# A gated layer's inverse deviation by Newton steps on VectorE, and two attentions whose ends are interleaved

## The chip, the cores and the metric

The kernel runs on one core of a Trainium2 chip. The metric is the device time in microseconds, median of the runs. PE is the matrix engine, DVE the vector engine, ACT the scalar engine, POOL the GpSimd engine; SP issues nearly all DMAs.

## What is computed

The input x has 4 batches of 512 rows of 256 numbers (f32). Four residual layers follow one another, each on the layer norm of x:

```
x = x + attn_a(ln(x))      # 16 heads of 128, causal softmax, biases
x = x + gated(ln(x))       # per head: o normalised by its own mean and variance, times silu(g)
x = x + attn_b(ln(x))      # 16 heads, low-rank queries, keys and values, rotary part, causal softmax
x = x + gated(ln(x))       # the same weights again
```

What matters of the gated layer (it mixes the four batches per position) is its end:

```
mu = mean(o, axis=-1); var = var(o, axis=-1)        # 16 heads of 16 numbers
o = (o - mu) / sqrt(var + EPS)
out = (silu(g) * o.reshape(b, l, d)) @ Wout
```

## The kernel before

The order of all work is written out by hand: every engine and every DMA queue runs its instructions in the order in which the program emits them, and the program waits only where data or a buffer demands it.

The main line is `attention_full`: 64 units (4 batches of 16 heads) in a loop of steps i = 0 to 66, a software pipeline. Step i scores unit i (four matmuls `score`, L282; mask and row maximum on DVE, L290; exponential on ACT, L293), transposes the probabilities of unit i-1 (32x32 blocks on DVE, L317, `turn`; then `carry`, L328 and L331: one DMA to DRAM, `way`, and four back), projects queries and keys of unit i+1 (L256), divides by the row sum on POOL (L308), multiplies by the values for unit i-2 (`mix`, L344) and adds a quarter of an older group of four heads to x (`output`, L366, L373). `load(i)` issues the weights of coming heads on SP, behind `carry`. So steps 64, 65 and 66 have no scores: they finish what is in the pipeline.

`attention_lowrank` is the second attention: 64 units of its own (`loop`, u = 0 to 66), each with four scores of growing width (L984), mask (L992), exponential (L995), division on POOL (L1011), transposes on PE (L1019) with copies to `probsT`, values (L1043), output (L1063). Its rotary parts are made by `rotated`: two products on DVE (L899, L900), two copies on ACT (L901, L902), then a shuffle on DVE (L905) and two sums on POOL (L906, L907). `compress_queries` (L915), `compress_keys` (L928), `compress_values` (L943) and `project` (L961) make its operands; `prologue(stage)` makes the first ones within steps 48 and 63 to 66 of the first attention, reading tables that `lowrank_weights` left in DRAM. PSUM has two buffers for such results (`ps_mm`).

Beside the main line run two lanes of generators, `norms` and `work`. Each call of `beside()` advances the first job of `norms`, or, when that is empty, of `work`, up to its next `yield`. A step of the first attention calls it four times (six for batches 2 and 3); a unit of the second four times (eight in the last batch). In `work` are the weights' preparation (`gated_weights`, `lowrank_weights`) and the gated layers, each as two halves of two row tiles that alternate yield by yield. A `norm` takes statistics on DVE (L132), makes `rstd` by a power and `shift` on POOL (L136 to L140), writes normalised rows `xn` on POOL (L146), turns them on PE (L154) and copies them to `xT` (L156). The last norm and last gated layer have nothing beside them.

The end of a half of a gated layer: squares on ACT (L675), their sum and the variance on DVE (L678, L679), then the power -1/2 in place, on POOL, in four pieces of 8 columns (L685), each with its own `yield`; the product with the gate on POOL (L690); the product with the inverse deviation on DVE (L692); transposes (L698) and the output product (L706). For the last gated layer alone, `by_power=False` takes a square root on ACT (L688) and a reciprocal on DVE (L689).

Of the kernel before, what the change touches and what calls it, by code (L numbers as in the profile page):

```python
# [10 lines left out]

F32 = mybir.dt.float32
AF = mybir.ActivationFunctionType
ALU = mybir.AluOpType
# [4 lines left out]
P = 128  # L19
# [16 lines left out]
def network(ctx: ExitStack, tc: tile.TileContext, ins: dict, out: bass.AP):  # L36
# [35 lines left out]

    slots = dict(bo=D, mask=S, probs_0=S, probs_2=3 * S, val0=D, val1=D, turns=2 * S)
    for i in range(2):
# [52 lines left out]
    def norm(b, take, extra=None):  # L127

        stats = lnpool.tile([P, NT, 6], F32, name="stats")
        mv = lnpool.tile([P, NT, 2], F32, name="mv")  # L130
        for t in range(NT):
            nc.vector.bn_stats(stats[:, t, :], x[b][t])  # L132
            nc.vector.bn_aggr(mv[:, t, :], stats[:, t, :])
            yield
        rstd = lnpool.tile([P, NT], F32, name="rstd")
        nc.gpsimd.tensor_scalar(rstd, mv[:, :, 1], EPS, None, ALU.add)  # L136
        nc.gpsimd.tensor_tensor(rstd, rstd, minus_half[:, :NT], ALU.pow)
        shift = lnpool.tile([P, NT], F32, name="shift")
        nc.gpsimd.tensor_tensor(shift, mv[:, :, 0], rstd, ALU.mult)
        nc.gpsimd.tensor_scalar(shift, shift, -1.0, 1.0, ALU.mult, ALU.mult)  # L140
        yield
        xT = new_xT()

        def normalise(t):
            xn = lnpool.tile([P, D], F32, name="xn")
            nc.gpsimd.tensor_scalar(  # L146
                xn, x[b][t], rstd[:, t : t + 1], shift[:, t : t + 1], ALU.mult, ALU.add
            )
            return xn

        def transpose(t, xn):
            pt = ps_tp()
            for c in range(DC):
                nc.tensor.transpose(pt[:, c * P : (c + 1) * P], xn[:, c * P : (c + 1) * P], ident)  # L154
# [19 lines left out]
    def attention_full(events, prologue):  # L174
# [218 lines left out]
        take_bias(0)()  # L393
        for i in range(n + 3):
            b, h = divmod(i, H)
# [19 lines left out]
            load(i)  # L415
            if i >= n - 1:
                prologue(i - n)
            beside(2 if b > 1 else 1)
# [14 lines left out]
            if 0 <= g < groups:  # L433
                for tt in range(t, NT if i == n + 2 else t + 1):
                    output(g, tt)


# [76 lines left out]

    def gated(layer, l, xT, xT_before, half, after, by_power=True):

# [163 lines left out]
        yield  # L680
        if by_power:
            step = 8
            for n in range(0, HT * H, step):
                part_ = var[:, n : n + step]
                nc.gpsimd.tensor_tensor(part_, part_, minus_half[:, :step], ALU.pow)  # L685
                yield
        else:
            nc.scalar.activation(var, var, AF.Sqrt)  # L688
            nc.vector.reciprocal(var, var)  # L689
        nc.gpsimd.tensor_tensor(o, o, gate, ALU.mult)  # L690
        yield
        nc.vector.tensor_tensor(og, og, var.unsqueeze(2).to_broadcast([P, HT * H, HDV]), ALU.mult)  # L692
        yield
# [51 lines left out]
    def lowrank_weights():  # L745
# [5 lines left out]
        for o in range(OCT):  # L751
            heads = slice(8 * o, 8 * o + 8)
            for to, tag, name in ((wqT, "w0", "b_wqT"), (wkT, "w1", "b_wkT"), (wvT, "gd", "b_wvT")):
                to.append(wide(tag, o, name[2:], S).rearrange("p (h r) -> p h r", r=RANK))
                nc.sync.dma_start(to[o], ins[name][:, heads, :])
            yield
            queries.append(wide("cx", o, "wqb"))
            wq.append(queries[o].rearrange("r (p s k) -> r p s k", p=4, s=2))
        wout = []
        places = [("kv1", 1), ("kv2", 0), ("kv2", 1), ("kv3", 0), ("kv3", 1), ("q", 0)]  # L760
        for i, place in enumerate(places):
            h0, h1 = 3 * i, min(H, 3 * i + 3)
            part = wide(*place, "wout", (h1 - h0) * D).rearrange("p (h d) -> p h d", d=D)
            nc.sync.dma_start(part, ins["b_wout"][:, h0:h1, :])
            wout += [part[:, h - h0, :] for h in range(h0, h1)]
            if i % 2:
                yield


        for i in range(2):  # L770
            nc.sync.dma_start(wkv[:, :, 0, i, :], ins["b_wkva"][:, :, :RANK])
            for block in range(2):
                for odd in range(2):
# [4 lines left out]
                    other = (1 - odd) * 32 + block * 16  # L778
                    nc.sync.dma_start(sin[rows], ins["c_sin"][RANK + other : RANK + other + 16])
                    nc.sync.dma_start(  # L780
                        wkv[:, :, 1, i, to : to + 16], ins["b_wkva"][:, :, RANK + at : RANK + at + 16]
                    )
                yield
        for o in range(OCT):
            for i in range(2):
                for block in range(2):
                    for odd in range(2):
# [4 lines left out]
                        )  # L792
                yield
            ps = ps_mm()
# [37 lines left out]
    def attention_lowrank(xTs, events):  # L832
# [14 lines left out]
        def load_tables():  # L847
            cos, sin, wkv = slot("wq0", "cos"), slot("wq1", "sin"), slot("wk0", "wkv")
            nc.sync.dma_start(wkv, tables[:, 2 * S :])
            nc.sync.dma_start(cos, tables[:, :S])  # L850
            nc.sync.dma_start(sin, tables[:, S : 2 * S])
            wq = slot("wv0", "wqb")
            nc.sync.dma_start(wq, to_queries)
            lw["cos"], lw["sin"] = (a.rearrange("p (i q) -> p i q", q=32) for a in (cos, sin))
            lw["wkv"] = wkv.rearrange("p (c a i r) -> p c a i r", c=DC, a=2, i=2)
# [9 lines left out]
        def buffers():  # L865
# [7 lines left out]
            lw["probs"] = {}  # L873
            for t in (0, 2, 3):
                probs_of(t)

        def probs_of(t):
            tag = ("probs_0", "zT0", "probs_2", "probs1")[t]
            lw["probs"][t] = slot(tag, f"probs{t}", (t + 1) * S).rearrange("p (i k) -> p i k", i=4)
# [3 lines left out]
        def more_buffers():  # L883
            probs_of(1)

# [5 lines left out]
        def rotated(first, second, ps):  # L891
# [3 lines left out]
            rank, straight = (p.rearrange("p (i q) -> p i q", q=32) for p in ps)  # L895
            both = slot(("wv1", "turns")[turns[0] % 2], "turns")
            turns[0] += 1
            t1, t2 = (both[:, i * S : (i + 1) * S].rearrange("p (i q) -> p i q", q=32) for i in range(2))
            nc.vector.tensor_tensor(t1, straight, lw["cos"], ALU.mult)  # L899
# [11 lines left out]
        def compress_queries(b):  # L911
            qas[b] = slot("wk1", "qa")
            ps = ps_mm()
# [157 lines left out]

        def prologue(stage):
            if stage == -2:
                load_first()
            elif stage == -1:
                load_tables()
            elif stage == 0:
                compress_queries(0)
                compress_keys(0)
                buffers()  # L1080
            elif stage == 1:
                compress_values(0)
                for p in range(2):
                    project(0, 0, p)()
            elif stage == 2:
                for p in range(2, 4):
                    project(0, 0, p)()

        pair_at = {(4, 1): 0, (5, 0): 1, (5, 2): 2, (6, 1): 3}
        output_at = {(1, 1): 0, (1, 3): 1, (3, 0): 2, (3, 2): 3}  # L1090
        compress_at = {(9, 2): compress_queries, (10, 3): compress_keys, (11, 3): compress_values}

        def loop():
            load_last()
            more_buffers()
            later = []
            for u in range(n + 3):
                octet, j = divmod(u, 8)
                b, jb = divmod(u, per_batch)
                events(u, b, jb)  # L1100
                for i in range(4):
# [43 lines left out]

    def then_gated(layer, l, after=None, by_power=True):
        def take(xT):
            gated_in[layer][l] = xT
            halves = [
                gated(layer, l, xT, gated_in[layer].get(l - 1), half, after, by_power)  # L1150
                for half in range(2)
# [5 lines left out]
    def during_full(i, b, h):  # L1157
# [4 lines left out]
        if (b, h) == (B - 1, 0):  # L1162
            assert (0, 0) in complete
            norms.add(norm(0, keep_lowrank(0)))
            prologue(-2)
# [17 lines left out]
    run(norm(B - 1, then_gated(1, B - 1, store, by_power=False)))  # L1183
    while work.jobs:
# [82 lines left out]
```

## Time and profile before

| | us |
|---|---|
| three runs | 1517.03, 1517.52, 1520.23 |
| median | 1517.52 |
| the profiled execution | 1520.02 |
| its span, first to last instruction | 1518.3 |
| PE busy | 1343.7 (89%) |
| DVE busy | 831.7 (55%) |
| POOL busy | 643.6 (42%) |
| ACT busy | 573.6 (38%) |

The mean granted clock of PE is 0.944 of full speed. Busy shares are means over stages: the first attention fills the first 850 us or so, the second the next 600, and the last gated layer the rest. A line of the profile names engine, source line, operation, what is written and what is read; a bracket gives the idle time before it and what ended it. SPq is SP's DMA queue. A wait is put down to the producer that came last.

### The profile page before, as it was taken

To read this page: it belongs to the slowest core of one execution; us is meant where nothing else is said; L and a number is where in the kernel's file an instruction comes from. 1 tells how busy PE (TensorE), PEld (TensorE's weight loads), DVE (VectorE), ACT (ScalarE), POOL (GpSimd) and SP (SyncE) were. 2 spreads that over 40 slices of the span, in tenths; PEclk is the share of its full clock that TensorE was granted. 3 is DMA by queue.
4 is the path that set the end of the run, shared out by engine and by line. 5 is a ranking of instruction groups with operands and counts; after the bars stand their busy time and mean duration, and the time that the engine had idled before them with its cause. 6 is when DMAs were issued, how large, how long until landed. Compare 5 with 4: busy or idle time off the path is not lost.

```text
span 1518.3 us, 16974 instructions
## 1 busy us (share of the span) xinstructions
PE 1343.7 (89%) x4984; PEld 778.2 (51%) x4984; DVE 831.7 (55%) x2460; ACT 573.6 (38%) x1593; POOL 643.6 (42%) x1027
## 2 busy tenths in 40 slices
PE   7969999999999999999995879996999799778771
PEld 3535556556556555655553535453645455435441
DVE  3533555554655566556483464974456556647327
ACT  3422333333333333333331245554355546434321
POOL 3311123221163235313346362867353666756624
PEclk9989999999999999999997899998899999989785
DMA  2776656554554535545353000000000000000000
GB/s 95 205 240 165 200 157 172 171 150 130 161 167 139 162 119 171 165 139 152 113 155 101 28 1 0 1 2 0 1 1 1 1 15 1 1 14 1 14 1 14
DMA packets 88284, 133.80 MB, mean 88 GB/s; under 512 B 16128, under 2 KB 69888, under 8 KB 88192
## 3 DMA queue, kind: packets, MB, share of 16 engines
q1 hardware_dynamic: 88192, 132.72, 29.6%
q8 instruction: 40, 0.66, 0.2%
q14 instruction: 52, 0.43, 0.1%
HBM read 86.29 MB, written 46.40 MB: 87 GB/s over the span
## 4 chain that ended last, share of the span: by engine, by line
PE 74%; DVE 9%; POOL 8%; DMA 3%; issue 3%; ACT 1%; SPq 1%; POOLq 0%; ACTq 0%; DVEq 0%
PE ps_mm L256 14%; PE ps_pz L344 9%; PE ps_sc L282 8%; PE ps_mm L243 7%; PE ps_mm L366 7%; PE ps_sc L984 6%; PE ps_mm L549 6%; PE ps_pz L1043 4%; PE ps_mm L1063 3%; PE ps_tp L1019 3%; PE ps_mm L706 2%; PE ps_mm L961 2%; POOL var L685 2%; POOL probs L1011 2%; PE ps_tp L154 1%
## 5 line engine op out<-in xcount | busy, mean ns | idle before, releaser
L308 POOL TENSOR_SCALAR probs<-probs,inv 128x128 f32<-128x128 f32 (+3 forms) x256 | 132.8, 537 | 492.4 <-DVE inv L305 444.5
L293 ACT ACTIVATE probs<-ps_sc,nmax 128x128 f32<-128x128 f32 (+3 forms) x256 | 134.8, 527 | 284.2 <-DVE nmax L290 260.8
L995 ACT ACTIVATE probs<-ps_sc,nmax 128x32 f32<-128x32 f32 (+15 forms) x256 | 124.6, 488 | 257.8 <-DVE nmax L992 185.8
L1011 POOL TENSOR_SCALAR probs<-probs,inv 128x32 f32<-128x32 f32 (+15 forms) x256 | 128.9, 521 | 146.0 <-DVE inv L1008 100.6
L984 PE MATMUL ps_sc<-kTb,qTb 128*128 128x160 f32 (+15 forms) x512 | 179.9, 443 | 9.5 <-ACT probs L995 8.2
L992 DVE CUSTOM_DVE_ANT_0 ps_sc<-ps_sc,mask_b 128x32 f32<-128x32 f32 (+15 forms) x256 | 112.9, 444 | 102.5 <-PE ps_sc L984 76.5
L282 PE MATMUL ps_sc<-kT,qT 128*128 128x128 f32 (+3 forms) x512 | 159.9, 435 | 1.9 <-DVE inv L305 0.9
L290 DVE CUSTOM_DVE_ANT_0 ps_sc<-ps_sc,mask_a 128x128 f32<-128x128 f32 (+3 forms) x256 | 126.4, 500 | 53.2 <-PE ps_sc L282 52.3
L344 PE MATMUL ps_pz<-probsT,v 128*128 128x512 f32 (+3 forms) x512 | 150.8, 438 | 3.1 <-DVE var L679 1.8
L984 PEld LDWEIGHTS ps_sc<-kTb,qTb 128*128 128x128 f32 x512 | 86.3, 201 | 105.4 <-issue 58.3
L344 PEld LDWEIGHTS ps_pz<-probsT,v 128*128 128x128 f32 x512 | 97.8, 192 | 82.4 <-issue 58.9
L256 PE MATMUL ps_mm<-xT,wk 128*128 128x512 f32 x256 | 122.8, 603 | 13.4 <-DMA wk<-in_a_wk_dram 13.4
L357 DVE TENSOR_SCALAR zT<-ps_pz,bias 128x512 f32<-128x512 f32 x64 | 48.0, 751 | 153.2 <-PE ps_pz L344 153.1
L243 PE MATMUL ps_mm<-wv,xT 128*128 128x512 f32 x256 | 122.4, 603 | 0.0
L256 PE MATMUL ps_mm<-xT,wq 128*128 128x512 f32 x256 | 121.7, 598 | 0.0
L366 PE MATMUL ps_mm<-wo,zT 128*128 128x256 f32 x512 | 120.8, 380 | 0.0
L317 DVE STREAM_TRANSPOSE squares<-probs 128x512 f32<-128x512 f32 (+3 forms) x256 | 115.0, 487 | 0.0
L1019 PE MATMUL ps_tp<-ident,probs 128*128 128x128 f32 x640 | 104.9, 289 | 11.1 <-ACT probsT L1028 7.2
L282 PEld LDWEIGHTS ps_sc<-kT,qT 128*128 128x128 f32 x512 | 86.2, 191 | 36.1 <-issue 26.9
L366 PEld LDWEIGHTS ps_mm<-wo,zT 128*128 128x128 f32 x512 | 94.0, 190 | 17.2 <-issue 6.7
L549 PE MATMUL ps_mm<-w_in,cx 128*128 128x512 f32 (+1 forms) x256 | 96.2, 509 | 6.0 <-DVE cx L540 4.7
L1019 PEld LDWEIGHTS ps_tp<-ident,probs 128*128 128x128 f32 x640 | 82.3, 152 | 37.3 <-issue 12.7
(141 smaller groups left out, 2020.2 us busy)
## 6 DMA issues: line engine op xcount, KB each, us to landing
way<-squares SPq DMA_DIRECT2D x64, 640.0 KB, 2.9
probsT<-way SPq DMA_DIRECT2D x256, 160.0 KB, 3.3
wv<-in_a_wv_dram SPq DMA_DIRECT2D x16, 512.0 KB, 5.1
wq<-in_a_wq_dram SPq DMA_DIRECT2D x32, 256.0 KB, 3.8
wk<-in_a_wk_dram SPq DMA_DIRECT2D x32, 256.0 KB, 3.9
wo<-in_a_wo_dram SPq DMA_DIRECT2D x16, 512.0 KB, 4.9
x<-in_x_dram SPq DMA_DIRECT2D x16, 128.0 KB, 3.4
out_dram<-x SPq DMA_DIRECT2D x16, 128.0 KB, 1.7
```

The lines of the kernel that those rows point to most:

```text
L243: nc.tensor.matmul(pv, lhsT=xTs[b][:, c, t * P : (t + 1) * P], rhs=wv[g][:, c, :], start=(c == 0), stop=(c == DC - 1),)
L256: nc.tensor.matmul(ps, lhsT=w[u // 2][:, c, (u % 2) * DH : (u % 2 + 1) * DH], rhs=xTs[b][:, c, :], start=(c == 0), stop=(c == DC - 1),)
L282: nc.tensor.matmul(ps[:, :m], lhsT=queries[u][:, t * P : (t + 1) * P], rhs=keys[u][:, :m], start=True, stop=True,)
L290: nc.vector.tensor_tensor_reduce(ps[:, :m], ps[:, :m], mask[:, S - m :], -1.0, 3.0e38, ALU.add, ALU.min, nmax[:, t : t + 1])
L293: nc.scalar.activation(pr[:, t, :m], ps[:, :m], AF.Exp, bias=nmax[:, t : t + 1], scale=-1.0, accum_out=total[:, t : t + 1],)
L308: nc.gpsimd.tensor_scalar(pr[:, t, :m], pr[:, t, :m], inv[:, t : t + 1], 1.0, ALU.mult, ALU.mult)
L344: nc.tensor.matmul(z[:, :, k:, :], lhsT=v[:, k, j * DH : (j + 1) * DH], rhs=pT[:, :, f : f + m, :], start=(k == 0), stop=(k == NT - 1),)
L366: nc.tensor.matmul(po[:, :D], lhsT=zTs[HG * g + i][:, t].rearrange("p i b -> p (i b)"), rhs=wo[g][:, i, :], start=(i == 0), stop=(i == HG ...
L549: nc.tensor.matmul(ps[:, : hi - lo], lhsT=cx[:, c, i * P : (i + 1) * P], rhs=w_in[:, c, lo:hi], start=(c == 0), stop=(c == DC - 1),)
L984: nc.tensor.matmul(ps, lhsT=q[:, m // 32 - 1].rearrange("p h q -> p (h q)"), rhs=kT[:, :m], start=True, stop=True,)
L1011: nc.gpsimd.tensor_scalar(probs[:, i, :m], probs[:, i, :m], inv[:, i : i + 1], 1.0, ALU.mult, ALU.mult)
L1019: nc.tensor.transpose(pt.rearrange("p (h i q) -> p h i q", h=4, i=4)[:, :, i, :], lw["probs"][t][:, i, k * P : (k + 1) * P], ident,)
```

## The change

Five edits.

- In `gated`, the powers on POOL and the square root on ACT are both replaced by a bit-level first guess of 1/sqrt(var) and three Newton steps on DVE: 2 + 9 instructions on 128x32 numbers for each half. The guess and the gate's product share a piece, and each Newton step ends in a `yield`, so a half has one piece fewer than with powers.
- In `norm`, the normalised rows are written by ACT in place of POOL.
- The first operands of the second attention are made some steps sooner (from step 61 on), and steps 65 and 66 of the first attention are run within the loop of the second, at its units 1 and 2. The norm of the last batch for the gated layer moves from u = 0 to u = 3.
- `lowrank_weights` yields after one to three DMA issues instead of after three to nine.
- Slots of the on-chip buffers get other names, so that the tables are in place sooner: `cos` and `sin` come by one DMA instead of two.

```diff
 def norm(b, take, extra=None):
-            nc.gpsimd.tensor_scalar(
-                xn, x[b][t], rstd[:, t : t + 1], shift[:, t : t + 1], ALU.mult, ALU.add
+            nc.scalar.activation(
+                xn, x[b][t], AF.Identity, bias=shift[:, t : t + 1], scale=rstd[:, t : t + 1]
             )
...
 def attention_full(events, prologue):
-        for i in range(n + 3):
+        def step(i):
...
-            if i >= n - 1:
-                prologue(i - n)
+            prologue(i)
...
+        for i in range(n + 1):
+            step(i)
+        return step
...
 def gated(layer, l, xT, xT_before, half, after):
-        if by_power:
-            step = 8
-            for n in range(0, HT * H, step):
-                part_ = var[:, n : n + step]
-                nc.gpsimd.tensor_tensor(part_, part_, minus_half[:, :step], ALU.pow)
-                yield
-        else:
-            nc.scalar.activation(var, var, AF.Sqrt)
-            nc.vector.reciprocal(var, var)
+        half_var, root = little("half_var", HT * H, "gap"), little("root", HT * H)
+        square = little("square", HT * H, "count")
+        nc.vector.tensor_scalar(half_var, var, -0.5, None, ALU.mult)
+        nc.vector.tensor_scalar(
+            root.bitcast(I32), var.bitcast(I32), -0.5, float(0x5F3759DF), ALU.mult, ALU.add
+        )
         nc.gpsimd.tensor_tensor(o, o, gate, ALU.mult)
         yield
-        nc.vector.tensor_tensor(og, og, var.unsqueeze(2).to_broadcast([P, HT * H, HDV]), ALU.mult)
+        for _ in range(3):
+            nc.vector.tensor_tensor(square, root, root, ALU.mult)
+            nc.vector.tensor_tensor(square, square, half_var, ALU.mult)
+            nc.vector.scalar_tensor_tensor(root, square, 1.5, root, ALU.add, ALU.mult)
+            yield
+        nc.vector.tensor_tensor(og, og, root.unsqueeze(2).to_broadcast([P, HT * H, HDV]), ALU.mult)
...
 def lowrank_weights():
                 nc.sync.dma_start(to[o], ins[name][:, heads, :])
-            yield
+                yield
...
-            if i % 2:
-                yield
+            yield
...
                     nc.sync.dma_start(sin[rows], ins["c_sin"][RANK + other : RANK + other + 16])
+                    yield
                     nc.sync.dma_start(
                         wkv[:, :, 1, i, to : to + 16], ins["b_wkva"][:, :, RANK + at : RANK + at + 16]
                     )
-                yield
+                    yield
...
                             wq[o][upper, :, i, to : to + 16], pe[:, 0, o, 1 - i, :, at : at + 16]
                         )
-                yield
+                        yield
...
 def load_tables():
-            cos, sin, wkv = slot("wq0", "cos"), slot("wq1", "sin"), slot("wk0", "wkv")
+            wkv, angles, wq = slot("wkv", "wkv"), slot("wv1", "angles"), slot("wv0", "wqb")
             nc.sync.dma_start(wkv, tables[:, 2 * S :])
-            nc.sync.dma_start(cos, tables[:, :S])
-            nc.sync.dma_start(sin, tables[:, S : 2 * S])
-            wq = slot("wv0", "wqb")
+            nc.sync.dma_start(angles, tables[:, : 2 * S])
...
 def prologue(i):
+            stage = i - H * B
+            if i == H * (B - 1):
                 load_first()
+            elif stage == -3:
+                load_tables()
+            elif stage == -2:
+                compress_queries(0)
+                compress_values(0)
             elif stage == -1:
-                load_tables()
-            elif stage == 0:
-                compress_queries(0)
                 compress_keys(0)
-                buffers()
-            elif stage == 1:
-                compress_values(0)
                 for p in range(2):
                     project(0, 0, p)()
-            elif stage == 2:
+            elif stage == 0:
+                buffers()
                 for p in range(2, 4):
                     project(0, 0, p)()
+                for t in (0, 2, 3):
+                    probs_of(t)
...
 def loop(former):
-            load_last()
             more_buffers()
...
+                if u in (1, 2):
+                    former(n + u)
+                    if u == 1:
+                        probs_of(1)
+                    else:
+                        load_last()
                 events(u, b, jb)
...
 def during_lowrank(u, b, jb):
         if u == 0:
-            norms.add(norm(B - 1, then_gated(0, B - 1)))
             norms.add(norm(1, keep_lowrank(1)))
+        if u == 3:
+            norms.add(norm(B - 1, then_gated(0, B - 1)))
...
-    attention_full(during_full, prologue)
-    loop()
+    loop(attention_full(during_full, prologue))
```

More of the change, by code (lines that the diff above doesn't have):

```diff
@@ L12 @@
 F32 = mybir.dt.float32
+I32 = mybir.dt.int32
 AF = mybir.ActivationFunctionType
@@ L70, in network @@
     ]
-    slots = dict(bo=D, mask=S, probs_0=S, probs_2=3 * S, val0=D, val1=D, turns=2 * S)
+    slots = dict(bo=D, mask=S, wkv=S, probs_2=3 * S, val0=D, val1=D, turn0=S, turn1=S)
     for i in range(2):
@@ L513, in network, with gated @@
     history = {}
-    def gated(layer, l, xT, xT_before, half, after, by_power=True):
+    def gated(layer, l, xT, xT_before, half, after):
         tiles = range(half * HT, (half + 1) * HT)
@@ L847, in load_tables @@
         def load_tables():
-            cos, sin, wkv = slot("wq0", "cos"), slot("wq1", "sin"), slot("wk0", "wkv")
+            wkv, angles, wq = slot("wkv", "wkv"), slot("wv1", "angles"), slot("wv0", "wqb")
             nc.sync.dma_start(wkv, tables[:, 2 * S :])
-            nc.sync.dma_start(cos, tables[:, :S])
-            nc.sync.dma_start(sin, tables[:, S : 2 * S])
-            wq = slot("wv0", "wqb")
+            nc.sync.dma_start(angles, tables[:, : 2 * S])
             nc.sync.dma_start(wq, to_queries)
-            lw["cos"], lw["sin"] = (a.rearrange("p (i q) -> p i q", q=32) for a in (cos, sin))
+            lw["cos"], lw["sin"] = (
+                angles[:, i * S : (i + 1) * S].rearrange("p (i q) -> p i q", q=32) for i in range(2)
+            )
             lw["wkv"] = wkv.rearrange("p (c a i r) -> p c a i r", c=DC, a=2, i=2)
@@ L873, in buffers @@
             lw["probs"] = {}
-            for t in (0, 2, 3):
-                probs_of(t)
         def probs_of(t):
-            tag = ("probs_0", "zT0", "probs_2", "probs1")[t]
+            tag = ("wq1", "zT0", "probs_2", "probs1")[t]
             lw["probs"][t] = slot(tag, f"probs{t}", (t + 1) * S).rearrange("p (i k) -> p i k", i=4)
@@ L883, in more_buffers @@
         def more_buffers():
-            probs_of(1)
             lw["probsT"] = [
@@ L895, in rotated @@
             rank, straight = (p.rearrange("p (i q) -> p i q", q=32) for p in ps)
-            both = slot(("wv1", "turns")[turns[0] % 2], "turns")
             turns[0] += 1
-            t1, t2 = (both[:, i * S : (i + 1) * S].rearrange("p (i q) -> p i q", q=32) for i in range(2))
+            t1, t2 = (
+                slot(tag, "turns").rearrange("p (i q) -> p i q", q=32)
+                for tag in (("turn0", "turn1"), ("wq0", "wk1"))[turns[0] % 2]
+            )
             nc.vector.tensor_tensor(t1, straight, lw["cos"], ALU.mult)
@@ L911, in compress_queries @@
         def compress_queries(b):
-            qas[b] = slot("wk1", "qa")
+            qas[b] = slot("wk0", "qa")
             ps = ps_mm()
@@ L1070, in output, with prologue @@
             nc.vector.tensor_tensor(x[b][t], x[b][t], po[:, :D], ALU.add)
-        def prologue(stage):
-            if stage == -2:
+        def prologue(i):
+            stage = i - H * B
+            if i == H * (B - 1):
                 load_first()
+            elif stage == -3:
[3 more added lines that the diff above has]
+                compress_values(0)
             elif stage == -1:
-                load_tables()
-            elif stage == 0:
-                compress_queries(0)
                 compress_keys(0)
-                buffers()
-            elif stage == 1:
-                compress_values(0)
                 for p in range(2):
                     project(0, 0, p)()
-            elif stage == 2:
+            elif stage == 0:
+                buffers()
                 for p in range(2, 4):
                     project(0, 0, p)()
+                for t in (0, 2, 3):
+                    probs_of(t)
         pair_at = {(4, 1): 0, (5, 0): 1, (5, 2): 2, (6, 1): 3}
@@ L1091, in attention_lowrank, with loop @@
         compress_at = {(9, 2): compress_queries, (10, 3): compress_keys, (11, 3): compress_values}
-        def loop():
-            load_last()
+        def loop(former):
             more_buffers()
@@ L1144, in finished, with then_gated @@
         yield
-    def then_gated(layer, l, after=None, by_power=True):
+    def then_gated(layer, l, after=None):
         def take(xT):
@@ L1149, in take @@
             halves = [
-                gated(layer, l, xT, gated_in[layer].get(l - 1), half, after, by_power)
+                gated(layer, l, xT, gated_in[layer].get(l - 1), half, after)
                 for half in range(2)
@@ L1164, in during_full @@
             norms.add(norm(0, keep_lowrank(0)))
-            prologue(-2)
     def during_lowrank(u, b, jb):
         if u == 0:
-            norms.add(norm(B - 1, then_gated(0, B - 1)))
             assert (0, 1) in complete
             norms.add(norm(1, keep_lowrank(1)))
+        if u == 3:
+            norms.add(norm(B - 1, then_gated(0, B - 1)))
         if b and jb == 4:
@@ L1178, in network @@
     prologue, loop = attention_lowrank(lowrank_in, during_lowrank)
-    attention_full(during_full, prologue)
-    loop()
+    loop(attention_full(during_full, prologue))
     while norms.jobs or work.jobs:
         beside()
-    run(norm(B - 1, then_gated(1, B - 1, store, by_power=False)))
+    run(norm(B - 1, then_gated(1, B - 1, store)))
     while work.jobs:
```

## The prediction, made blind

> **What bounds it now.** I read the page's slices first: PE is at nine tenths or more through slices 4 to 21 (a slice is 38 us), and falls in slice 3, in slices 22 to 24 and again from 28 on.
>
> ```profile
> PE   7969999999999999999995879996999799778771
> POOL 3311123221163235313346362867353666756624
> PEclk9989999999999999999997899998899999989785
> ```
>
> So PE is the bound, and time is lost where it stands still. From windows of 2 us, PE stands idle some 11 us and works 2.6 us too long at half clock in 100 to 130 us; 19.2 and 6.6 us in 790 to 856; 13.7 and 5.8 us in 856 to 900; 72 and 24 us in 900 to 1440; 41 us in the end from 1454. From 130 to 790 it idles only 1.3 us: nothing saved there on another engine counts.
>
> Then PE's timeline and the DMA queue's own, at the first hole:
>
> ```profile
> 99.89 1.15 PE L796 MATMUL ps_mm<-wkT,wqT 128*64 128x64 f32 x16
> 112.11 3.75 PE L256 MATMUL ps_mm<-xT,wk 128*128 128x512 f32 x4 [11.08 <-DMA wk<-in_a_wk_dram]
> ...
> 102.89 0.54 SPq L328 DMA_DIRECT2D way<-squares  x1
> 106.11 1.75 SPq L331 DMA_DIRECT2D probsT<-way  x4
> 107.90 0.55 SPq L184 DMA_DIRECT2D wk<-in_a_wk_dram  x1
> ```
>
> wk is issued last in a queue that had held the second attention's weights (a dozen issues of about half a us each) ahead of the round trip of the probabilities.
>
> Windows of 10 us at the change of attentions: the first has no more heads, the second has not begun (its first scores run at 854.86).
>
> ```profile
> 800.00:810.00 10.00, 6.58 (x12) 3.02 (x13) 1.21 (x2) 1.16 (x2) 3.70 (x3) 0.83 0.83 250
> 820.00:830.00 10.00, 4.35 (x7) 1.30 (x8) 4.20 (x7) 1.16 (x2) 4.74 (x5) 0.50 0.00 0
> ```
>
> Columns: PE, weight load, DVE, ACT and POOL busy, then clock, DMA share, GB/s.
>
> Last, in the second attention, PE's waits (first two lines, 1250 to 1350 us) and POOL's timeline behind them:
>
> ```profile
> PE ps_tp L698 <- DVE o L692: 9.3, 1, 9.3
> PE ps_tp L154 <- POOL xn L146: 8.3, 1, 8.3
> ...
> 1325.96 6.46 POOL L685 TENSOR_TENSOR var<-var,minus_half 128x8 f32<-128x8 f32 x4
> 1332.38 1.25 POOL L906 TENSOR_TENSOR qTb<-turns 64x512 f32<-64x512 f32 x1
> 1333.71 1.26 POOL L907 TENSOR_TENSOR qTb<-turns 64x512 f32<-64x512 f32 x1
> 1335.05 1.64 POOL L685 TENSOR_TENSOR var<-var,minus_half 128x8 f32<-128x8 f32 x1
> ```
>
> PE is in order: its transposes of o wait for four powers, rotations and another power on POOL.
>
> **The sum**, in us, against the profiled execution (1520.02, span 1518.3, so 1.7 around it). I take the changes from the median of 1517.52.
>
> *A. Spread weight DMAs.* Same DMAs, but at most three per step instead of three to nine. The hole of 11.08 and its cold clock (2.6) are the prize, 13.7. One unit of the first attention lasts some 10.4; SP spends on it 0.34 + 3 (trip of way) + 1.75 + 0.55 and about 0.3 for wv and wo, so 6; four steps with about six issues of 0.5 add 3, which makes 9 and fits. The large weights still share the DMA engines (337 to 393 GB/s at 76 to 84), so about 2 to 3 remain: **-11** (0 to -13.7). The lane runs out some eight units later, still before the first norm of the gated layer.
>
> *B. Interleaving.* Scores of the second attention start at 854.86. Counted anew from 779.6, the start of step 62: that step gets the queries' and values' compression (1.88 + 1.89 of PE) on its 9.5, so 13.3. Step 63 has PE 14.4, but DVE 15.6: scores and turns 4.4, three rotations of 0.69 + 0.68 + 0.75 = 6.4, 1.3 for zT, x and inv, and 3.5 of gated work; so 16. Step 64 has PE 8.3 with waits of 2 for ps_mm, DVE 10.4: 11. Scores then start at about 820, 34 sooner. To be done later, beside units 1 to 3: mix 2.3, five outputs 9.0 and the rest of gated(0, 2) 5.2, together 16.5. It fills some 6 of the 13.7 idle in 856 to 900 and spares about 3 of cold clock: -34 + 16.5 - 9 = -26.5, taken as **-26** (-10 to -34). The moved DMAs: table loads (three issues of 0.43) go ahead of step 62's round trip, at a time when no wk or wq is left to load; the 4.08 that PE waited for wkv goes. The two wvo loads stand behind the outputs of step 66 as before (14.1 on SP now), and nothing PE needs soon is queued behind them. The norm of batch 3 is put off by three units, but the gated work behind it starts only when both norms are done, as now. Memsets and renamed slots: the same instructions, so 0; their cover is the PE work of step 64, and without it they cost under 2.
>
> *C. No power on POOL.* 56 powers of 1.64 (90.6 in all) go. PE waits of 3.56 + 2.50 (1058 to 1067), 9.30 (1330) and 7.24 (1415) end on POOL's queue with powers in it: 22.6; half clock behind them costs 10.2 (windows of 2 us: busy time times one minus clock). What is late next is the product with gate on POOL (1.26), issued six steps earlier than its reader: **-30** (-15 to -33).
>
> *D. Norm rows on ACT.* 64 x 0.55 leave POOL. No row shows such an ACTIVATE; near ones are tanh 128x256 at 0.416 and identity with a bias operand, 128x512, at 0.687, so about 0.5, 32 in all. [...] I go by POOL's timeline: the rows then don't stand behind rotations.
>
> ```profile
> 1028.66 0.20 POOL L139 TENSOR_TENSOR shift<-mv,rstd 128x4 f32<-128x4 f32 x1
> 1029.12 1.26 POOL L906 TENSOR_TENSOR qTb<-turns 64x512 f32<-64x512 f32 x1
> 1030.45 1.26 POOL L907 TENSOR_TENSOR qTb<-turns 64x512 f32<-64x512 f32 x1
> 1031.83 1.09 POOL L146 TENSOR_SCALAR xn<-x,rstd,shift 128x256 f32<-128x256 f32 x2
> ```
>
> That is worth 2.7 of PE's wait of 4.42 there and the 1.64 after it, the same (4.40, 1.48) at 1178; at 1307 (8.32) rstd itself stood behind rotations, so only 0.5. With 2 of clock: 10.7; taken at **-8** (0 to -12), since the chain up to shift stays on POOL.
>
> *E. Price on DVE and ACT.* Newton: 11 instructions of 128x32 for each of 16 halves. Near rows: L606, eight independent ones in 1.73, so 0.216; dependent ones L619 to L621 begin 0.21 to 0.31 apart. I take 0.27, 3.0 a half. [...] Ten halves lie after 790: 30 of DVE, where DVE is 319 of 540 busy and PE hardly idles at 65% of DVE (1200 to 1300): **+4** (0 to +15; all 30 without that cover). On ACT xn now waits for shift, with exponentials and copies of probsT queued behind it, and PE waits for those: 14 norms beside attention, most covered: **+5** (0 to +25).
>
> *F. The end.*
>
> ```profile
> 1506.21 0.60 DVE L679 TENSOR_SCALAR var<-var 128x32 f32<-128x32 f32 x1
> 1506.73 0.73 DVE L689 RECIPROCAL var<-var 128x32 f32<-128x32 f32 x2
> 1507.37 1.22 DVE L692 TENSOR_TENSOR o<-o,var 128x512 f32<-128x512 f32 x2
> ```
>
> From the end of the last L679 (1506.81) to L692 pass 0.56 now; 22 Newton instructions at 0.27 make 5.9, nothing beside them: +5.4 [...]. The third row on ACT stands behind a copy of xT: about +0.1. **+5.5** (+3 to +7). The table load of the square root was hidden (it ends 0.8 ahead of L688's second use).
>
> Sum: -11 - 26 - 30 - 8 + 4 + 5 + 5.5 = -60.5; 1517.5 - 60.5 = **1457**.
>
> **Rivals.** *Little from the change of attentions and new waits* (chance 0.24): DVE was 73 to 94% busy in 750 to 800, and rotations and Newton steps are put there; each pair of ps_mm waits for DVE. B falls to -12, C to -18 as other waits take over: -11 - 12 - 18 - 8 + 14.5 = -34.5, so **1483**. For it: DVE's rows; against: PE 97% busy at 65% of DVE.
> *More* (0.14): A, B, C, D at their far ends, E at 2, F at 5: -13.7 - 34 - 33 - 12 + 7 = -86, so **1432**. For it: 24 us of half clock in 900 to 1440 shrink with every hole.
> *Slower* (0.03): ACT held by xn. If POOL delivers shift late, exponentials stop and PE with them, also in the first attention, where PE is full and nothing waits for xn now. 14 norms at 8.3 (the longest present wait) are 116: 1457 - 5 + 116, about **1568**. It decides from some 4.7 a norm ((60.5 + 5) / 14). Against it: between 130 and 790 PE never waits for a norm row, so shift comes in time there.
> *Doesn't do what it says* (0.01): a spread lane whose wk still comes last, and Newton as late as the powers: within 0.2%.
>
> **Numbers.** Forecast 0.58, 1445 to 1470; the rivals as above. The range takes in somewhat over half of the first rival and half of the better case (from 1438, between 1445 and 1432), and leaves out some 0.2: 1438 to 1486. A measurement of this kernel tells about 0.2% (3 us) from no change: faster 0.96, same 0.01, slower 0.03.
>
> **What would show it.** A: no PE wait for wk over 3 us before 130. B: first L984 near 820 to 825, slices 22 and 23 at eight or nine. C: no wait of the transposes of o over 2 us before the end. D: waits for xn after 900 sum to about half of their 20. F: 5 to 6 us between variance and L692 in the end. It is wrong if DVE shows over 80% after 900 with PE idle, if the exponentials wait for xn, or if the first scores come after 835.

## The result, and the profile after

The changed kernel takes 1514.72 us (median of 20 runs), the kernel before 1520.33 beside it: a ratio of 0.9958 [0.9944, 0.9972], a gain of 6 us where 60 were forecast. In the profiled execution the span falls from 1518.3 to 1510.9 and PE is busy for 1343.2 us as before; its idle time falls by 7 us only.

The slices of the page after, to be laid over those of before:

```profile
PE   6989999999999999999997879889898998688861
POOL 2311221221222233212245263853434355436323
PEclk9999999999999999999998999999999999889885
```

Counted as in the prediction, the hole at slice 22 is half filled (5 to 7), slices 23 to 25 read 8, 7, 9 as before, and from slice 29 on the digits of PE add to 88 where they added to 89, though POOL has become emptier. Line numbers after are a few higher than before. The first hole, on PE's timeline, and the windows at the change of attentions:

```profile
103.33 1.19 PE L257 MATMUL ps_mm<-xT,wk 128*128 128x512 f32 x1 [6.17 <-DMA wk<-in_a_wk_dram]
```

```profile
800.00:810.00 10.00, 8.44 (x27) 4.23 (x26) 8.11 (x18) 3.71 (x8) 6.83 (x6) 1.00 0.45 133
820.00:830.00 10.00, 6.89 (x25) 4.61 (x24) 9.55 (x28) 1.00 (x5) 4.81 (x13) 0.84 0.45 119
```

The wait for wk is 6.17 in place of 11.08. The second attention's scores begin at 825.6, 29 us sooner (the edit moved `score` to L990), and DVE is nearly full around it (9.55 of 10 us). Two units on, the lead is 10. Where the rest went shows in PE's timeline from the first scores on, and in the windows behind them (columns as in the prediction):

```profile
828.82 0.49 PE L990 MATMUL ps_sc<-kTb,qTb 128*128 128x128 f32 x2 [2.42 <-ACT probs L1001]
...
833.71 1.18 PE L155 MATMUL ps_tp<-ident,xn 128*128 128x128 f32 x4 [4.40 <-ACT xn L147]
...
858.86 0.93 PE L155 MATMUL ps_tp<-ident,xn 128*128 128x128 f32 x4 [2.92 <-ACT xn L147]
```

```profile
825.60:835.00 9.40, 2.58 (x14) 2.02 (x13) 5.64 (x23) 2.84 (x11) 1.83 (x6) 0.74 0.00 0
835.00:845.00 10.00, 10.00 (x47) 7.65 (x47) 4.09 (x14) 4.51 (x14) 1.57 (x7) 0.91 0.14 53
845.00:855.00 10.00, 10.00 (x48) 8.38 (x47) 5.08 (x19) 0.62 (x3) 0.53 (x2) 1.00 0.07 17
```

PE waits once for its first scores' exponentials, behind the queue on DVE, and twice for rows of norms that fall among the first units; in between it is full, above all with what was postponed to units 1 and 2. DVE is no longer full here. Last, PE's waits from 1250 to 1350:

```profile
PE ps_tp L155 <- ACT xn L147: 9.1, 1, 9.1
PE ps_tp L1025 <- ACT probsT L1034: 5.2, 3, 2.9
PE ps_mm L553 <- DVE cx L544: 4.5, 1, 4.5
```

The 9.3 behind powers (L698 before) is gone. In its place stand waits for copies (`probsT`) and for the gated layer's convolution (`cx`), and the long one for xn is still there (8.3 before).

### The profile page after: what moved, and what is told of

Its sections match the earlier page's. It is cut to its first block, busy times and chain, and to the rows that moved or that the text cites. A ratio compares the mean times of both kernels' runs of the same rounds, so it can differ in the third digit from the quotient of the medians.

```text
span 1510.9 us, 17025 instructions
## 1 busy us (share of the span) xinstructions
PE 1343.2 (89%) x4984; PEld 773.8 (51%) x4984; DVE 871.5 (58%) x2634; ACT 604.9 (40%) x1654; POOL 517.7 (34%) x907
## 5 line engine op out<-in xcount | busy, mean ns | idle before, releaser
L990 PE MATMUL ps_sc<-kTb,qTb 128*128 128x160 f32 (+15 forms) x512 | 178.0, 440 | 21.7 <-ACT probs L1001 20.2
L998 DVE CUSTOM_DVE_ANT_0 ps_sc<-ps_sc,mask_b 128x32 f32<-128x32 f32 (+15 forms) x256 | 113.2, 444 | 124.0 <-PE ps_sc L990 88.2
L990 PEld LDWEIGHTS ps_sc<-kTb,qTb 128*128 128x128 f32 x512 | 84.6, 197 | 116.2 <-issue 56.0
L553 PE MATMUL ps_mm<-w_in,cx 128*128 128x512 f32 (+1 forms) x256 | 100.5, 527 | 14.5 <-DVE cx L544 7.4
```

What stands on the lines that cost most here:

```text
L553: nc.tensor.matmul(ps[:, : hi - lo], lhsT=cx[:, c, i * P : (i + 1) * P], rhs=w_in[:, c, lo:hi], start=(c == 0), stop=(c == DC - 1),)
L990: nc.tensor.matmul(ps, lhsT=q[:, m // 32 - 1].rearrange("p h q -> p (h q)"), rhs=kT[:, :m], start=True, stop=True,)
L998: nc.vector.tensor_tensor_reduce(ps, ps, lw["mask"][:, S - m :], -1.0, 3.0e38, ALU.add, ALU.min, nmax[:, i : i + 1])
```

## The experiments

A word used below: the *place* of the background work. The lanes advance one yield per quarter of a unit (two in the last batch), so the program's text alone decides beside which quarter of which unit of the second attention each background step is emitted. As a mark I take the variance (L678) of the third batch's second gated layer, first half, and write 60.2 for unit 60, quarter 2. The mark stands for all gated work of the second layer, which moves with it. The *stretch* is the time from unit 32 to unit 56 of the second attention in the one profiled execution of each kernel, from reciprocal to reciprocal of the row sum (L1008).

S is edit A, the spread DMAs; I the interleaving with its buffers; N Newton; X the rows on ACT.

| kernel | ratio to before [95%] | place | stretch, us |
|---|---|---|---|
| before | 1 | 60.2 | 224.2 |
| e1_spread: S | 0.9942 [0.9924, 0.9961] | 60.2 | 225.1 |
| e2_inter: I | 1.0019 [1.0006, 1.0033] | 60.3 | 225.3 |
| e3_newton: N | 0.9925 [0.9899, 0.9951] | 59.2 | 234.2 |
| e4_xn: X | 1.0048 [1.0032, 1.0064] | 60.2 | 221.8 |
| e5_ns: N+S | 0.9846 [0.9820, 0.9872] | 59.2 | 233.6 |
| e6_nsi: N+S+I | 0.9927 [0.9902, 0.9952] | 59.3 | 243.3 |
| e7_nsx: N+S+X | 0.9868 [0.9844, 0.9892] | 59.2 | 231.2 |
| after: N+S+I+X | 0.9958 [0.9944, 0.9972] | 59.3 | 240.9 |
| e8_double: N, six steps | 1.0123 [1.0100, 1.0146] | 59.2 | 244.4 |
| e9_early: N+S, operands early | 0.9811 [0.9789, 0.9834] | 59.2 | 234.7 |
| e10_lane: N+S+I, norm moved | 0.9774 [0.9748, 0.9801] | 60.2 | 224.2 |
| e11_nslane: N+S, norms in the new order | 0.9859 [0.9835, 0.9883] | 59.2 | 234.0 |
| e12_two: N+S, two steps | 0.9844 [0.9822, 0.9865] | 58.3 | 241.9 |
| e13_blank: N+S+I, 4 empty steps | 0.9915 [0.9896, 0.9933] | 60.1 | 237.9 |
| e14_nsblank: N+S, 4 empty steps | 0.9897 [0.9872, 0.9922] | 60.0 | 240.2 |
| e15_newtonkeep: N, place kept | 0.9864 [0.9846, 0.9882] | 60.2 | 222.8 |
| e16_afterlane: after, norm moved | 0.9792 [0.9771, 0.9812] | 60.2 | 221.2 |
| e17_blank7: N+S+I, 7 empty steps | 0.9800 [0.9775, 0.9824] | 60.2 | 224.0 |
| e18_blank6: N+S+I, 6 empty steps | 0.9785 [0.9760, 0.9810] | 60.2 | 226.2 |

### Each edit alone

Two theories at this point. The *parts theory*: each edit has its own gain and its own price, and is worth less than its term even alone. The *rival*: alone, each edit is worth its forecast, and the edits get in each other's way. Each kernel is the one before with one edit's hunks of the diff, for instance e4:

```
-            nc.gpsimd.tensor_scalar(
-                xn, x[b][t], rstd[:, t : t + 1], shift[:, t : t + 1], ALU.mult, ALU.add
+            nc.scalar.activation(
+                xn, x[b][t], AF.Identity, bias=shift[:, t : t + 1], scale=rstd[:, t : t + 1]
             )
```

> The kernel before with the weight DMAs spread alone. Parts theory (each part has its own gain and its own price, and both show alone): the PE wait for wk falls from 11.1 us to about 6 and the half clock with it, so -5 to -8 us. Rival (the parts get in each other's way and are worth their forecast alone): -11 us, and no wait for wk over 3 us.

> The kernel before with the interleaving and its slots alone. Parts theory: first scores of the second attention some 30 us sooner, but most of it given back within the next four units: -8 to -13 us. Rival: -26 us as forecast, since rotations are not held by Newton steps on DVE nor exponentials by rows on ACT.

> The kernel before with Newton steps in place of powers alone. Parts theory: the waits of 22 us behind powers go, but Newton instructions that meet a two-input operation of POOL last 1.3 us and hold the masks behind them; +3 in the end: between -10 and 0 us. Rival: -20 to -25 us, as forecast with the end counted.

> The kernel before with the norms' rows on ACT alone. Parts theory: four to six new PE waits of 2.1 us in the first attention, little gained in the second: +4 to +10 us. Rival: -3 to -8 us as forecast.

Measured, at 1520 us to a ratio of 1: S -9, I +3, N -11, X +7. Their sum, -10, is near the -6 of the whole, so no collision between edits is needed yet to explain it; three of the four are not worth their terms even alone, and I is worse than either theory had it. For X the trace shows why. ACT's and PE's timeline of e4 in the first attention (row L146 is xn, L265 a copy of queries, L293 the exponential):

```profile
427.87 0.69 ACT L265 ACTIVATE qT<-ps_mm,bq 128x512 f32<-128x512 f32 x1 [0.45 <-PE ps_mm L256]
...
429.90 0.69 ACT L293 ACTIVATE probs<-ps_sc,nmax 128x512 f32<-128x512 f32 x1 [1.08 <-DVE nmax L290]
...
430.58 1.08 ACT L146 ACTIVATE xn<-x,shift,rstd 128x256 f32<-128x256 f32 x2
...
431.22 0.93 PE L154 MATMUL ps_tp<-ident,xn 128*128 128x128 f32 x4 [2.15 <-ACT xn L146]
```

The rows stand behind an exponential that itself waits for DVE, and PE, full until then, waits 2.15. Four such waits in the first attention make 8.6 us, where before had none.

### The edits stacked, and Newton doubled

> Newton steps and spread weight DMAs together, rows on POOL, no interleaving. If the two add up (-11 and -9 alone): -20 us against the kernel before, about 0.987. If what one saves the other gives back: -12 us.

> The whole change but for the rows, which stay on POOL. If the powers on POOL were what spoiled the interleaving (a wait of 9.3 us behind powers just after the change of attentions), it gains 8 to 12 us over Newton and spread alone: about -30 us. If the interleaving is worth nothing in itself: -17 us (-11 - 9 + 3).

> The whole change but for the interleaving. If rows on ACT cost their 7 us here too: -13 us. If they cost only where POOL has powers to run: -20 us.

> Newton alone, with six steps in place of three (the last three change nothing in the result): 9 more DVE instructions for each half. If those beside attention are hidden, only the end pays, 18 x 0.166 = 3 us over Newton alone: about -8 us against before. If Newton instructions hold the masks of the scores on DVE: 8 to 12 us over Newton alone, about 0.

S and N add up (-23 us). X on top costs 3, and 5 with the interleaving in. The interleaving on top of N and S takes 12 us back, where it cost 3 alone and was expected to gain or to cost 3: that was the open question. e8 repeats each step's three instructions:

```
             nc.vector.scalar_tensor_tensor(root, square, 1.5, root, ALU.add, ALU.mult)
+            nc.vector.tensor_tensor(square, root, root, ALU.mult)
+            nc.vector.tensor_tensor(square, square, half_var, ALU.mult)
+            nc.vector.scalar_tensor_tensor(root, square, 1.5, root, ALU.add, ALU.mult)
             yield
```

Its 144 further instructions cost 30 us over e3, 0.21 each, of which 18 in the end account for about 3: the added ones are not hidden at all, and cost about three times what either theory gave them. Where POOL rotates at the same time they are far from 0.2. The timeline of after:

```profile
1029.70 0.20 DVE L695 TENSOR_TENSOR square<-root 128x32 f32<-128x32 f32 x1
1029.89 1.26 POOL L912 TENSOR_TENSOR qTb<-turns 64x512 f32<-64x512 f32 x1 [5.07 <-DVE square L695]
1029.93 1.27 DVE L696 TENSOR_TENSOR square<-square,half_var 128x32 f32<-128x32 f32 x1
...
1031.23 1.26 POOL L913 TENSOR_TENSOR qTb<-turns 64x512 f32<-64x512 f32 x1
1031.24 1.30 DVE L697 SCALAR_TENSOR_TENSOR root<-square,root 128x32 f32<-128x32 f32 x1
...
1032.47 0.68 DVE L1061 COPY zTb<-ps_pz 128x512 f32<-128x512 f32 x1
1033.07 0.55 DVE L998 CUSTOM_DVE_ANT_0 ps_sc<-ps_sc,mask_b 128x384 f32<-128x384 f32 x1
...
1034.43 2.43 PE L990 MATMUL ps_sc<-kTb,qTb 128*128 128x480 f32 x3 [2.15 <-ACT probs L1001]
```

L696 and L697 last as long as the POOL sum beside them, a copy and the mask L998 are queued behind them, the exponential behind the mask, and PE waits 2.15.

### Which piece of the interleaving costs

Theories: the early operands; the interleaved steps; the new order of two norms. e9 has the operands early but steps 65 and 66 ahead of the loop, and the norms as before:

```
-        for i in range(n + 1):
+        for i in range(n + 3):
             step(i)
-        return step
...
-                if u in (1, 2):
-                    former(n + u)
...
```

e10 has N, S and the whole of I, with one norm put back behind the other; e11 is N+S with the order of the lines marked "-" here; e12 has `range(2)` for the Newton steps:

```
-        if u == 0:
-            assert (0, 1) in complete
-            norms.add(norm(1, keep_lowrank(1)))
         if u == 3:
             norms.add(norm(B - 1, then_gated(0, B - 1)))
+            assert (0, 1) in complete
+            norms.add(norm(1, keep_lowrank(1)))
```

> Newton and spread DMAs, with the operands of the second attention's first units made early (tables, low-rank queries, keys, values and first projections one to three steps sooner, in the new buffers), but steps 65 and 66 of the first attention ahead of the loop and the two norms in the order of before. Newton and spread alone stand at 0.985, with the interleaving at 0.993. If the early operands cost the time (they stretch unit 62 to 63 by 10 us and nothing is gained from their being early), this stands at 0.991 to 0.994. If the interleaved steps or the order of the norms cost it, this is at 0.982 to 0.986: as Newton and spread alone, or up to 4 us better, because the scores no longer wait for their operands.

> Newton, spread and the whole interleaving, with one thing put back: the norm of the second sequence for the second attention stands behind the last norm of the first attention's results, as in the kernel before, both from unit 3 of the second attention. If the order of the two norms costs the 12 us (its statistics fall between the first scores, and the gated work of the last sequence begins later against the attention), this goes back to 0.984 to 0.987. If it is the early operands or the interleaved steps, it stays at 0.991 to 0.995.

> Newton and spread with no interleaving, but with the order of the norms that the change has (the second sequence's norm from unit 0 of the second attention, the last of the first attention's results from unit 3). If that order costs the time, 0.990 to 0.994; if not, 0.983 to 0.987. A result in the same direction as the run without the order is needed before the order is called the cause.

> Newton and spread with two Newton steps in place of three: it leaves out the third step, and the deviation is less exact (about 5e-6 in place of rounding). Doubling the steps from three to six cost 30 us, 10 us a step. If each step costs what the doubling says, this gains 10 us over three steps: 0.978. If the first steps are hidden beside attention and only the added ones were too many, as the prediction had it (4 us for all three between the attention's units, and 1 us at the end), it gains 1 to 3 us: 0.983.

e9 and e11 clear the operands and, on N and S, the order by itself; e10 gains 23 us by moving one norm. Counted out in the program, e10 also shifts everything later: both lanes run empty for seven steps (three within step 66, four at unit 2), and the background work then stands seven steps later (59.3 to 60.2 at two steps a quarter). e12 decides nothing, since dropping a step moves the place too.

### Place or order

```
         if u == 3:
             norms.add(norm(B - 1, then_gated(0, B - 1)))
+            norms.add(iter([None] * 4))
```

is e13 (7 in e17, 6 in e18; in e14 the same 4 on N+S, behind both norms at u == 0). e15 puts a second `yield` after the gate product (L690) of N. e16 is after with e10's edit.

> Newton, spread and interleaving, with the norms in the order of the change, and only four empty steps put into the queue of norms at unit 3 of the second attention, so that all later background work stands one unit later (the variance of the third sequence's second gated layer at unit 60, quarter 1, in place of unit 59, quarter 3). Without them this stood at 0.993; with the second norm put behind the first, at 0.977. If the place of the background work against the units is the cause, this gains 10 to 20 us, to 0.979 to 0.986. If the order of the norms at the seam is the cause, it stays at 0.991 to 0.995.

> Newton and spread without interleaving (0.985), with the same four empty steps. If the place of the background work sets the time in general, this moves too, by 5 us or more in either direction; down to 0.978 if one unit later is the better place for this part of the program. If the place matters only with the interleaving, it stays at 0.982 to 0.987.

> Newton alone (0.9925), with an empty step after the gate product, so that a gated half has as many steps as with the powers and the background work stands where it stood before. If Newton's dropped step cost something by shifting the rest, this is faster than 0.9925 by 5 us or more (the prediction's C, E and F come to 20.6 us, or 0.9864). If the shift is worth nothing here, it stays at 0.990 to 0.995, and what is missing of the 20.6 us is the Newton instructions' own cost.

> The whole change with one norm moved: the second sequence's norm stands behind the last norm of the first attention's results, from unit 3. The whole change stood at 0.9958; Newton, spread and interleaving with this move at 0.977, and the rows on ACT cost 3 to 7 us. If the place of the background work is what took the gain, this is at 0.979 to 0.984. If the rows on ACT set the time by themselves here, it stays above 0.990.

> Newton, spread and interleaving, norms in the order of the change, with seven empty steps at unit 3 in place of four. From the last gated layer of the first kind on, every variance and norm then stands in the same quarter of the same unit as in the run with the moved norm (0.977), while the first twenty units keep the order of the change. If the place of the background work takes the time, this is at 0.977 to 0.984 (the run with the moved norm, with up to 8 us left from its better seam). If the order of the norms takes it, this stays at 0.990 to 0.995.

> The same with six empty steps: from unit 48 on, where two steps stand beside each quarter, both halves of a gated layer have their variance in one quarter (unit 60, quarter 2 twice) and not in two neighbouring ones. If it counts that the halves are apart, this is 8 us or more slower than with seven, at 0.988 to 0.993, near the runs with none and with four, which have both halves in one quarter as well. If it is the place to within a quarter that counts, it is as with seven, within 4 us. If the order of the norms takes the time, both are at 0.990 to 0.995.

e14 moves as well, by 8 us and for the worse: the place matters without the interleaving too, and later isn't better as such. e13 alone spoke for the order. e17 overturned that: with the order unchanged, seven empty steps reach e10's time, and six do as well, so it doesn't count whether both halves fall in one quarter. Between four and six steps lie 20 us. The stretch says the same over all 20 kernels: 221 to 226 with the place at 60.2 or later, 231 to 244 earlier, whatever else was changed. It holds 11.7 of the 18 us between the profiled executions of e13 and e18. The stretch of e13 and then of e18 in windows (columns as in the prediction):

```profile
1126.50:1364.50 238.00, 201.19 (x877) 113.83 (x876) 145.83 (x466) 111.37 (x320) 112.62 (x180) 0.93 0.02 5
```

```profile
1123.20:1349.50 226.30, 197.33 (x878) 112.96 (x877) 147.48 (x468) 110.69 (x319) 113.63 (x176) 0.93 0.02 6
```

In e13 it is the same work to within 2 us on DVE, ACT and POOL, and takes 11.7 us more: what differs is what stands beside what. One meeting of many, in e13's timeline, four units from 1231.7 that took 39.4 us against 33.8 in e18:

```profile
1234.13 1.31 DVE L537 SCALAR_TENSOR_TENSOR cx<-xT,conv,cx 128x256 f32<-128x256 f32 x2 [0.59 <-POOL cx L531]
...
1235.86 0.42 ACT L1001 ACTIVATE probs<-ps_sc,nmax 128x192 f32<-128x192 f32 x1 [2.32 <-POOL cx L531]
...
1236.87 1.88 DVE L537 SCALAR_TENSOR_TENSOR cx<-xT,conv,cx 128x256 f32<-128x256 f32 x2
...
1240.37 0.63 PE L1025 MATMUL ps_tp<-ident,probs 128*128 128x128 f32 x4 [1.65 <-ACT probsT L1034]
```

The gated layer's convolution (L537) stands on DVE ahead of the masks of a unit that rotates its queries at the same time; ACT waits 2.32 (its exponential starts as the mask ends; the profile names POOL's part of the convolution, which ends at the same time), and PE later 1.65. In e18 the same convolution stands some 3 us later in its unit.

## Why the prediction was wrong, step by step

Two things failed: the sum had no term for the place, and its term B took 9 us of postponed work for hidden that was not; D is a smaller miss. On the first: the prediction asked of each moved step what it issues, but not what the *number* of yields does to all that follows. The list of edits said that a half has one piece fewer with Newton; that moves the mark from 60.2 to 59.2, and the change of attentions with its norm at u = 0 leaves it at 59.3. Moving one norm in the whole change (e16) puts it back to 60.2 and takes the ratio from 0.9958 [0.9944, 0.9972] to 0.9792 [0.9771, 0.9812]: some 25 us, nearly half of the missing 55. That this is the place, and not the order of the norms, is shown by e17 and e18: they leave the order, and gain 19 and 22 us over e6 where e10 gains 23. The few us between them are within the noise. Which meeting of steps has which share is not settled.

With the place held, the terms stand so. C and B rest on these lines besides: PE's waits for o (900 to 1440, in before and in e15), and for rows of a norm at the first scores of e2 (820 to 862):

```profile
PE ps_tp L698 <- DVE o L692: 20.1, 3, 9.3
```

```profile
PE ps_tp L703 <- DVE o L697: 5.7, 2, 3.8
```

```profile
PE ps_tp L154 <- POOL xn L146: 9.3, 1, 9.3
```

- **A**, forecast -11: e1 -9. The mechanism was right. The wait for wk that is left is 6.17 us, not the 2 to 3 of the sum.
- **C with the Newton part of E, and F**, forecast -30 + 4 + 5.5 = -20.5: e15 gives -20.7 [-23.4, -17.9]. The mechanism of C is in its trace: PE's waits for o fall from 20.1 to 5.7, though 3.8 and not under 2 is left at once. The sum holds, but its split isn't shown, and the match may be luck. By e8's 0.21 for each instruction, the 126 step instructions of the 14 halves ahead of the last two would cost some 26 and not 4, and the powers' removal would be worth more than 30. e12 would have told, but its place moved. With the place let go, e3 has only -11: 9 us of Newton's gain went to the dropped yield.
- **F** by itself: the 22 instructions of the end run from 1496.05 to 1499.71, 3.66 us, 0.166 from start to start, against the 0.27 taken. From unit 63 to the end the time grows by 3.2 (80.0 to 83.2 in e3), not 5.5.
- **B**, forecast -26: the mis-sized term. e9 over e5 is worth -5 us [-11, 0], and e10, e17 and e18 stand at 0.979 on average, where S and N with the place held add to 0.9864 - 0.0058 = 0.981: -3 us for the whole interleaving. The start came as forecast (825.6, and 823.1 in e2, for 820). The credit did not: the sum gave 16.5 back and took 9 of those for hidden or spared. In e2, which has nothing else and stands at 60.3, 21 of 32 us were gone two units on: about what the postponed work in full and 6 us more of waiting make (PE waited 10.6 us between its first scores and there, 4.5 in before). Most of the waiting is for the norm of u = 0, which falls among the first scores (9.3 in e2, 4.40 in after). The prediction looked at when the gated work behind that norm starts, and not at the norm itself. e2 still had 9 us at unit 8 and lost them by the last unit; why is open.
- **D with the ACT part of E**, forecast -8 + 5 = -3: +7 alone, +3 [-2, +9] on N+S, and +3 [-2, +8] in e16 over e10. The trade on ACT was mis-sized on both sides. In the first attention four waits of 2.15 appear where the prediction counted on "shift comes in time": shift does, ACT's queue doesn't. In the second, PE waits 21.5 us for xn between 866 and 1444, where it waited 25.7 (877 to 1454): a sixth less, not half.

With the place held the sum is -9 - 21 - 3 + 3 = -30, and e16 measures -32. This is bookkeeping and no test, since B and D are themselves read from e10, e16, e17 and e18. By it, of the 55 us that were missing the place has some 20 to 25, B 23, D with its ACT part 6 and A 2.

Of the rivals, the first had B in the right direction (-12, still too much), but its cause, DVE at the change of attentions, only in small part: the scores start as forecast, and behind them 2.42 us of PE's waits go back to DVE and 7.3 to rows of norms. For C, E and F it had -8.5 (without the ACT part) where e15 gives -20.7, and it lacked the place as well. The slower one had its mechanism in the trace (rows held on ACT), at 2 us in each of four norms, below its 4.7.

N, S and I with the norm moved or six empty steps (e10, e18) beat both kernels by some 2%; the rows on ACT add nothing to that.

## What to carry to other kernels

Where background work advances by yields beside a main line, an edit that adds or drops a yield moves all later work: count out the place first, and compare an edit's worth only with the place held (an empty step issues nothing and does that). A late change of a few steps should be tried in both directions before an edit is judged. A start that is brought forward pays for the postponed work in full, as in e2 (21 of 32 us gone two units on), unless the next stage has been shown to have room for it; look also at what else falls among its first steps.

## What was not expected of the hardware

Two-input Newton instructions of 128x32 on DVE that run beside a TENSOR_TENSOR on POOL last 0.99 us on average (13 of them, median 1.21), those clear of one 0.21 (131, median 0.19), between 400 and 1515 us of after: up to some six times the duration (L697 at 1031.24 takes 1.30 beside L913 on POOL). The cause is not shown, and no run here isolates the effect. The trace of before had it already: L606, the row by which the prediction priced a Newton instruction at 0.216, also has two inputs of 128x32, and its 40 instructions last from 160 to 1262 ns, the longest beside a sum of the rotary part on POOL. The row on ACT takes 0.589 us (median, L147 of after), on POOL 0.549 (L146 of before); the prediction took about 0.5.
